# First cross-attention of a four-layer decoder: key steps issued in pairs instead of one by one

## The chip, the cores and the metric

The kernel runs on one core of a Trainium2 chip. The metric is the device time of one execution in microseconds (us). The core's engines work side by side, each through its own instructions in order, and wait for one another by semaphores: TensorE (PE, with its weight loads PEld) multiplies matrices into PSUM; VectorE (DVE) and ScalarE (ACT) read PSUM and SBUF; GpSimd (POOL) works on SBUF alone; SyncE (SP) issues most transfers. Changes of under 0.2% cannot be told from no change here.

## The reference, cut to what matters

A decoder of four layers; each has self-attention, cross-attention over a context of 6404 keys, and a feed-forward block. The change is in the cross-attention of the first layer alone: 1024 queries, 16 heads of 64, all 6404 keys, float32.

```python
qw = (q_in @ Wq + bq).reshape(B, M, HEADS, QSIZE)
kw = (k_in @ Wk + bk).reshape(B, N, HEADS, QSIZE)
vw = (v_in @ Wv + bv).reshape(B, N, HEADS, KSIZE)
a = jnp.einsum('bmhd,bnhd->bhmn', qw, kw) / jnp.sqrt(jnp.float32(QSIZE))
a = jnp.where(key_mask[:, None, None, :], a, -jnp.inf)
a = jax.nn.softmax(a, axis=-1)
o = jnp.einsum('bhmn,bnhd->bmhd', a, vw).reshape(B, M, HEADS * KSIZE)
return o @ Wo + bo
```

Here q_in is the normalised x, and k_in and v_in are the context; the result is added to x.

## The kernel before

The work of the stage (`l0_xattn`, L675 on) is cut into 64 **units**: 16 heads by 4 blocks of W = 256 queries. The keys lie in two halves of 3202 (HALF), each half on 64 of the 128 partitions of kS. A unit goes through the keys in NSTEP = 13 **steps**; a step takes two runs of 123 or 124 keys (`key_step`, L574) from each half, four in all, so its scores are 123 or 124 partitions by 1024 columns (two banks of PSUM, tile s, two buffers); such a set of scores is called a **strip** below.

The softmax runs in two passes. In the first, a step's scores are made, joined to a running maximum, and copied to SBUF (tile p, 18 buffers). When all 13 are there the maximum over the keys is found; in the second pass, 15 steps later (NS + LAG), each slot has its maximum subtracted, is raised to the exponential, summed, and multiplied with the values. So one turn of the loop over a, in `l0_xattn`, issues scores of one unit and the second pass of the unit before. The instructions of a turn:

- `scores` (PE, all at helper line L275): for each of two runs, and in each of both halves of the rows, a float32 product of kS and q with 256 columns (two records each), then a bfloat16 product of the mask row `drop` with ones, which adds a large negative number to dropped keys. The two halves of the rows work as separate 64-row tiles.
- `lowered` (DVE L771): slot plus the negated maxima, which stand in PSUM (tile neg). `raised` (ACT L776): the exponential in place. `summed` (POOL L785): the slot is added to tot; after the last step tot is folded once, to 512 columns (toth, L788).
- `kept`: the running maximum (DVE L735, reads s and most), then the copy from s to p (ACT L737).
- after the last step of a unit `halved` (DVE L742) folds the maximum to 512 columns; one turn later `turned` transposes it on PE (L751) and reduces it on DVE (L754), and `spread` (PE L763), two turns after the halving, puts the negated maxima of the queries on all partitions.
- `weighted` (PE, L275): the values of the step before, acc<-p,v, in 64-column tiles; eight records. After a unit's last step `taken` (ACT L809) copies acc to oT, and two steps later `onto` makes the denominators (m<-ones,toth, eight records) and the output product (m<-w_head,oT); DVE takes the reciprocal (rd, L826) and adds the result to x (L829).

Beside this stand, at set turns, the keys of the next head (`head_keys`, seven chunks, ACT L598), its queries (two, ACT L700), and in the last unit of every second head the values of the next two heads (`pair_values`, one a step, ACT L617). These, `turned` and `onto` share two PSUM buffers of tile m.

The order is written out by hand: every instruction of the loop goes through `pin` or `matmul`, which keep it in program order on its engine. `pool.tile` hands out the buffers of a tag in turn; an instruction that writes a buffer waits until the earlier readers are done.

Of the kernel before, what the change touches and what calls it, by code (L numbers as in the profile page):

```python
# [218 lines left out]
class Decoder:  # L219
# [354 lines left out]
    def key_step(self, i):  # L574

        n = 124 if i < 2 else 123
        return (248 * i if i < 2 else 496 + 246 * (i - 2)), n
# [8 lines left out]
    def head_keys(self, w):  # L586

        nc, H = self.nc, self.HALF
        k = self.keys_pool.tile([P, H], F32, tag="kS", name="kS", bufs=2)

        def chunks(psum):
            for c in range(0, H, BANK):
                n = min(BANK, H - c)
                m = psum()
                for s in range(2):
                    self.matmul(m[64 * s:64 * s + 64, :n], lhsT=w[:, 128:192], rhs=self.ctxT[:, s * H + c:s * H + c + n],
                                start=True, stop=True, tile_position=(0, 64 * s))
                self.pin(nc.scalar.activation(k[:, c:c + n], m[:, :n], AF.Identity, bias=w[:, 321:322]))  # L598
                yield

        return k, chunks
# [7 lines left out]
    def pair_values(self, w, i, m):  # L609

        c, n = self.key_step(i)
        v = self.keys_pool.tile([P, 4, P], F32, tag=f"v{i}", name="v", bufs=1)
        for s in range(2):
            for j in range(2):
                a = s * self.HALF + c + j * n
                self.matmul(m[:n, (2 * s + j) * P:(2 * s + j + 1) * P], lhsT=self.ctxT[:, a:a + n], rhs=w, start=True, stop=True)
# [3 lines left out]
    def first_keys(self, ps, pool):  # L620
# [10 lines left out]
        self.drop = kp.tile([P, self.HALF], BF16, tag="drop", name="drop")  # L631
        nc.gpsimd.memset(self.drop, 0.0)
        for s in range(2):
            nc.sync.dma_start(out=self.drop[64 * s:64 * s + 1, :],
                              in_=line.rearrange("t p -> (t p)")[s * self.HALF:(s + 1) * self.HALF][None, :])
        self.one16 = kp.tile([P, self.WQ], BF16, tag="one16", name="one16")
        nc.gpsimd.memset(self.one16, 1.0)
# [37 lines left out]
    def l0_xattn(self):  # L675
# [6 lines left out]
        NH, NB, NS, W, H = 16, S // self.WQ, self.NSTEP, self.WQ, self.HALF  # L682
        LAG, LIVE = 2, 18
        units = NH * NB
        with tc.tile_pool(name="b", bufs=2) as pool, tc.tile_pool(name="b_ps", bufs=2, space=PSUM) as ps0:
# [25 lines left out]
            def scores(a):  # L711

                u, i = divmod(a, NS)
                _, k, q = heads[u // NB]
                c, n = self.key_step(i)
                qs = slice(u % NB * W, u % NB * W + W)
                s = ps.tile([P, 2, BANK], F32, tag="s", name="s")
                for j in range(2):
                    ks = slice(c + j * n, c + j * n + n)
                    for lhs, rhs, first in ((k, q[:, qs], True), (self.drop, self.one16, False)):  # L720
                        for t in range(2):
                            r = slice(64 * t, 64 * t + 64)
                            mm(s[:n, t, j * W:(j + 1) * W], lhsT=lhs[r, ks], rhs=rhs[r, :], start=first, stop=not first)
                return s

            def kept(a, s):

                u, i = divmod(a, NS)
                n = self.key_step(i)[1]
                p = pool.tile([P, 2 * BANK], F32, tag="p", name="p", bufs=LIVE)  # L730
                flat = s.rearrange("p t c -> p (t c)")
                if i == 1:
                    most[u] = pool.tile([P, 2 * BANK], F32, tag="most", name="most")
                if i:
                    pin(nc.vector.tensor_tensor(most[u][:n], flat[:n], (most[u] if i > 1 else slots[a - 1])[:n], ALU.max))  # L735
                slots[a] = p
                return lambda: pin(nc.scalar.copy(p[:n], flat[:n]))  # L737

            def halved(u):

                mh = pool.tile([P, BANK], F32, tag="half", name="half", bufs=1)
                pin(nc.vector.tensor_tensor(mh[:124], most[u][:124, 0:BANK], most[u][:124, BANK:], ALU.max))  # L742
                del most[u]
                most[u] = mh

            def turned(u):

                m = psum()
                for b in range(2):
                    for j in range(2):  # L750
                        pin(nc.tensor.transpose(m[:, b * W + j * P:b * W + j * P + 124],  # L751
                                                most[u][:124, j * W + b * P:j * W + (b + 1) * P], self.ident[:124, :124]))
                r = pool.tile([P, 2], F32, tag="r", name="r")
                pin(nc.vector.tensor_reduce(r, m.rearrange("p (b j k) -> p b j k", b=2, j=2)[:, :, :, :124], AX.XY, ALU.max,  # L754
# [11 lines left out]
            def lowered(b):  # L766

                u, i = divmod(b, NS)
                n = self.key_step(i)[1]
                p = slots[b][:n].rearrange("p (t c) -> p t c", c=W)  # L770
                pin(nc.vector.tensor_tensor(p, p, negs[u][:n, None, :W].to_broadcast([n, 4, W]), ALU.add))  # L771

            def raised(b):

                n = self.key_step(b % NS)[1]
                pin(nc.scalar.activation(slots[b][:n], slots[b][:n], AF.Exp))  # L776

            def summed(b):

                u, i = divmod(b, NS)  # L780
                n = self.key_step(i)[1]
                if i == 1:
                    tots[u] = pool.tile([P, 2 * BANK], F32, tag="tot", name="tot")
                if i:
                    pin(nc.gpsimd.tensor_tensor(tots[u][:n], slots[b][:n], (tots[u] if i > 1 else slots[b - 1])[:n], ALU.add))  # L785
                if i == NS - 1:
                    th = pool.tile([P, BANK], F32, tag="toth", name="toth", bufs=1)
                    pin(nc.gpsimd.tensor_tensor(th[:124], tots[u][:124, 0:BANK], tots[u][:124, BANK:], ALU.add))  # L788
                    tots[u] = th

            def weighted(b):

                u, i = divmod(b, NS)
                n = self.key_step(i)[1]
                h = u // NB
                if i == 0:
                    accs[u] = ps.tile([P, BANK], F32, tag="acc", name="acc")
                v, p, e = values[h // 2][i], slots[b], 64 * (h % 2)
                for j in range(2):
                    for t in range(2):  # L800
                        at = (2 * t + j) * W
                        mm(accs[u][64 * t:64 * t + 64, :W], lhsT=v[:n, 2 * t + j, e:e + 64], rhs=p[:n, at:at + W],
                           start=i == 0 and j == 0, stop=i == NS - 1 and j == 1, tile_position=(0, 64 * t))
                slots.pop(b - 1, None)
# [7 lines left out]
            def onto(u, oT):  # L812
# [4 lines left out]
                for b in range(2):  # L817
                    for j in range(2):
                        mm(m[:, W + b:W + b + 1], lhsT=th[:124, j * W + b * P:j * W + (b + 1) * P], rhs=self.ones[:124, 0:1],
                           start=j == 0, stop=j == 1)  # L820
                for b in range(2):
                    mm(m[:, b * P:(b + 1) * P], lhsT=oT[:, b * P:(b + 1) * P], rhs=w[:, 192:320], start=True, stop=True)
                rd = pool.tile([P, 2], F32, tag="rd", name="rd")

                def add():
                    pin(nc.vector.reciprocal(rd, m[:, W:W + 2]))  # L826
                    for b in range(2):
                        x = self.x[:, u % NB * 2 + b, :]
                        pin(nc.vector.scalar_tensor_tensor(x, m[:, b * P:(b + 1) * P], rd[:, b:b + 1], x, ALU.mult, ALU.add))  # L829

                return add

            keys, asked, vw = iter(()), iter(()), None
            out = None
            total = units * NS
            for a in range(total + NS + LAG + 3):
                u, i = divmod(a, NS)
                b = a - NS - LAG
                ub, ib = divmod(b, NS)
                h, at = divmod(a, NB * NS)  # L840
                if a < total and h + 1 < NH:
                    if at == 2:
                        w = self.head_weights(h + 1)
                        k, gen = self.head_keys(w)
                        keys = gen(psum)
                        qn, asked = queries(w)
                        heads[h + 1] = (w, k, qn)
                    if at >= 6 and at % 5 == 1:
                        next(keys, None)
                    if at in (44, 48):  # L850
                        next(asked, None)
                s = scores(a) if a < total else None
                if 0 <= b < total:
                    lowered(b)
                    raised(b)
                    summed(b)
                copy = kept(a, s) if a < total else None
                if copy:
                    copy()
                if a < total and i == NS - 1:  # L860
                    halved(u)
                if u > 0 and i == 0 and u <= units:
                    turned(u - 1)
                if 0 <= b - 1 < total:
                    weighted(b - 1)
                    pu, pi = divmod(b - 1, NS)
# [1147 lines left out]
```

## Time and profile before

| what | us |
|---|---|
| median of 3 runs | 5793.36 (5789.67 to 5799.3) |
| the profiled execution | 5792.23 |
| its span, first to last instruction | 5790.1 |
| stretch of the first cross-attention, from the first p copy on | 284 to 2633 |

| engine, whole span | busy us | share |
|---|---|---|
| PE | 5373.4 | 93% |
| PEld | 2453.1 | 42% |
| DVE | 3767.8 | 65% |
| ACT | 3801.8 | 66% |
| POOL | 2256.3 | 39% |

Costs of one instruction in the stretch, by the view of groups and the tile views:

| line, engine | what | mean ns | times |
|---|---|---|---|
| L735 DVE | most<-s,most, 1024 columns | 1224 | 704 |
| L771 DVE | p<-p,neg, 1024 columns | 1210 | 832 |
| L737 ACT | p<-s, 1024 columns | 1011 | 832 |
| L776 ACT | p<-p (exponential), 1024 columns | 1059 | 832 |
| L785 POOL | tot<-p,tot, 1024 columns | 2398 | 704 |
| L788 POOL | toth<-tot, 512 columns | 1274 | 64 |
| L742 DVE | half<-most, 512 columns | 1276 | 64 |

And of the same kinds elsewhere in the profile: L451 DVE p<-s,neg, 512 columns, 692; L452 ACT exponential, 512 columns, 630; L456 POOL tot<-tot,p, 512 columns, 1266.

How to read it: a share of busy time is a mean over the whole kernel, of which the first cross-attention is some 40%. The line L275 is that of a helper, so PE's products are told apart by their tiles. Durations of PE overlap with one another, so its costs are read as distances from start to start. The chain of waits ends in later layers and passes through this stage by PE.

### The profile page before, as it was taken

The numbers are of one execution on the slowest core, as the hardware profiler recorded it, in microseconds if no ns is written. First come the engines' busy times: TensorE is split into PE (matmuls) and PEld (weight loads), VectorE is DVE, ScalarE is ACT, GpSimd is POOL, SyncE is SP. The second block draws the span as 40 slices with busy tenths as digits, with TensorE's granted clock in tenths as the row PEclk, the third lists the DMA queues.
The fourth block names the chain that finished last, engine by engine and source line by source line (L and its number), as shares of the span: only waits on it lengthen the run. The fifth ranks groups of instructions, "written<-read, shape, count | busy, mean of one in ns | idle before, by whom it ended". The sixth has DMA issues, their size and how long they took to land. (4 is left out here: it accounts for less than half of the span.)

```text
span 5790.1 us, 89326 instructions
## 1 busy us (share of the span) xinstructions
PE 5373.4 (93%) x36760; PEld 2453.1 (42%) x36760; DVE 3767.8 (65%) x4507; ACT 3801.8 (66%) x4975; POOL 2256.3 (39%) x1089
## 2 busy tenths in 40 slices
PE   6899999999999999998999589999997699999999
PEld 3355555565656565654854232111144111111136
DVE  5588888888888888882354622000035999999913
ACT  2477777778787777772223258999901188888772
POOL 1078887878788888782325301000001000000000
PEclk8899999999999999998999779999998599999999
DMA  3000000000000000001000133000033000000000
GB/s 106 1 1 2 3 2 3 2 3 2 3 3 3 2 2 2 1 1 49 6 11 1 62 91 95 10 9 1 9 120 103 1 8 16 16 9 1 1 12 26
DMA packets 67724, 115.74 MB, mean 20 GB/s; under 512 B 10748, under 2 KB 50018, under 8 KB 65908
## 3 DMA queue, kind: packets, MB, share of 16 engines
q1 hardware_dynamic: 66740, 106.76, 5.9%
q8 instruction: 288, 4.72, 0.3%
q10 hardware_dynamic: 576, 3.28, 0.2%
q14 instruction: 120, 0.98, 0.1%
HBM read 78.56 MB, written 31.42 MB: 19 GB/s over the span
## 5 line engine op out<-in xcount | busy, mean ns | idle before, releaser
L785 POOL TENSOR_TENSOR tot<-p,tot 123x1024 f32<-123x1024 f32 x704 | 1688.3, 2398 | 309.1 <-ACT p L776 265.7
L275 PE MATMUL acc<-p,v 123*64 123x256 f32 (+4 forms) x9896 | 1326.2, 458 | 25.1 <-ACT oT L809 20.3
L1382 DVE TENSOR_REDUCE mx<-m 128x2 f32<-128x1024 f32 (+4 forms) x928 | 1027.1, 1157 | 94.1 <-PE m L275 84.5
L275 PE MATMUL s<-q,kS 64*123 64x256 f32 (+1 forms) x6656 | 1031.1, 401 | 11.9 <-ACT p L737 11.3
L776 ACT ACTIVATE p<-p 123x1024 f32<-123x1024 f32 (+1 forms) x832 | 881.0, 1059 | 210.4 <-DVE p L771 187.2
L771 DVE TENSOR_TENSOR p<-p,neg 123x1024 f32<-123x1024 f32 (+1 forms) x832 | 1006.3, 1211 | 16.6 <-PE neg L763 9.9
L737 ACT COPY p<-s 123x1024 f32<-123x1024 f32 (+1 forms) x832 | 841.0, 1011 | 252.9 <-DVE most L735 232.8
L1454 ACT ACTIVATE p<-s 128x512 f32<-128x512 f32 (+4 forms) x1620 | 819.4, 589 | 230.7 <-PE s L275 229.6
L735 DVE TENSOR_TENSOR most<-s,most 123x1024 f32<-123x1024 f32 x704 | 861.4, 1224 | 149.1 <-PE s L275 148.1
L1451 ACT ACTIVATE p<-s 128x1024 f32<-128x1024 f32 x918 | 844.0, 1183 | 31.1 <-PE s L1446 31.0
L275 PEld LDWEIGHTS acc<-p,v 123*64 123x64 f32 (+3 forms) x9896 | 456.4, 121 | 594.7 <-issue 373.3
L275 PEld LDWEIGHTS s<-q,kS 64*123 64x123 f32 (+1 forms) x6656 | 492.3, 182 | 406.5 <-issue 226.6
L1425 PE MATMUL acc<-p,v 128*8 128x512 f32 (+2 forms) x3672 | 622.1, 596 | 0.0
L275 PE MATMUL m<-kP,qP 64*128 64x512 bf16 (+4 forms) x1856 | 369.3, 394 | 111.8 <-DVE mx L1382 57.3
L275 PE MATMUL s<-one,drop 64*123 64x256 bf16 (+1 forms) x3328 | 458.7, 269 | 0.0
L275 PE MATMUL s<-qP,kP 64*128 64x512 bf16 (+4 forms) x1620 | 380.1, 384 | 7.9 <-ACT p L1454 5.3
L785 POOL TENSOR_TENSOR tot<-p 124x1024 f32<-124x1024 f32 x64 | 151.9, 2373 | 352.3 <-ACT p L776 352.3
L1446 PE MATMUL s<-qP,kP 48*128 48x512 bf16 (+2 forms) x1836 | 280.3, 383 | 5.7 <-ACT p L1451 4.9
L281 DVE COPY oT<-acc 128x512 f32<-128x512 f32 x14 | 9.7, 690 | 400.4 <-PE acc L1425 391.1
L275 PEld LDWEIGHTS <-qP 64*128 64x128 bf16 x1856 | 122.3, 96 | 326.5 <-issue 259.0
L400 POOL MEMSET mpad<- 128x512 f32 x2 | 1.1, 526 | 639.9 <-PE m L1535 603.1
L275 PEld LDWEIGHTS <-drop 64*123 64x123 bf16 (+1 forms) x3328 | 231.3, 132 | 43.8
(478 smaller groups left out, 4902.0 us busy)
## 6 DMA issues: line engine op xcount, KB each, us to landing
kd<-part SPq DMA_DIRECT2D x156, 128.0 KB, 1.9
wb<-expert_weights SPq DMA_DIRECT2D x30, 512.0 KB, 3.8
kP<-kd SPq DMA_DIRECT2D x24, 512.0 KB, 4.6
kP<-kd SPq DMA_DIRECT2D x48, 192.0 KB, 4.7
w_expert<-in_Y_w SPq DMA_DIRECT2D x8, 768.0 KB, 4.3
qd<-part SPq DMA_DIRECT2D x36, 128.0 KB, 1.9
qP<-qd SPq DMA_DIRECT2D x16, 256.0 KB, 5.6
ctxT<-in_ctxT ACTq DMA_DIRECT2D x4, 800.5 KB, 7.4
```

The costliest lines, as they stand in the source:

```text
L275: return self.tc.keep_in_program_order(self.nc.tensor.matmul(*a, **k))
L281: self.nc.vector.tensor_copy(out, in_)
L735: pin(nc.vector.tensor_tensor(most[u][:n], flat[:n], (most[u] if i > 1 else slots[a - 1])[:n], ALU.max))
L737: return lambda: pin(nc.scalar.copy(p[:n], flat[:n]))
L771: pin(nc.vector.tensor_tensor(p, p, negs[u][:n, None, :W].to_broadcast([n, 4, W]), ALU.add))
L776: pin(nc.scalar.activation(slots[b][:n], slots[b][:n], AF.Exp))
L785: pin(nc.gpsimd.tensor_tensor(tots[u][:n], slots[b][:n], (tots[u] if i > 1 else slots[b - 1])[:n], ALU.add))
L1382: nc.vector.tensor_reduce(mx[:, t, 2 * pair:2 * pair + 2, c:c + 1], m[:, :, :b - a], AX.X, ALU.max)
L1425: matmul(acc[32 * j:32 * j + v.shape[3], off:], lhsT=v[:n, t, 4 * g + j, :], rhs=ws[j][:n, :BANK - off], start=t == 0, stop=t == nkt - 1, ...
L1446: matmul(ss[j][:n, :w], lhsT=kP[pair][r, t * P:t * P + n], rhs=qP[pair][r, hs], start=True, stop=not diag)
L1451: nc.scalar.activation(p2[:n], both[:n], func)
L1454: nc.scalar.activation(pp[j][:n, :w], ss[j][:n, :w], func)
```

## The change

**Pairs.** The 13 steps of a unit become seven groups: six pairs and the last alone, g0 to g6; bg0 to bg6 are the groups of the second pass. A turn of the loop issues the scores of both steps of a group, then the lowering, the maxima and copies, the raise, the sum, and then the values of both steps of a group. The lag is counted in groups: the second pass comes 8 turns (LAG = NG + 1) after the scores, the values one turn after the raise. Key chunks stand in turns 3, 4, 5, 10, 11, 12 and 17 of a head's 28, queries in 18 and 19; the values of the next heads are made two a turn.

**Slots.** A pair has one slot of 2048 columns (tag pp, 9 buffers); the last step has one of 1024 (tag p, 2 buffers). Lowering, raise and sum take a whole slot in one instruction. The running maximum has one buffer instead of two, and so has tot.

**Mask.** All steps have 124 keys a run (KT). The padding of the first half's last step runs into the second half's keys and is masked; ctxT gets 22 zero columns for the second half's. `drop` holds the mask of a strip's two runs in two rows, and `one16` has ones where row and run agree, so that one product of 512 columns masks a strip. It stands first in the strip, before the float32 products.

**Sums.** tot has 2048 columns and is folded three times, to 1024, 512 and 256 columns; the denominators take two products instead of four.

**Order.** The transposes of the maximum stand between the two strips of the next unit's first group; `spread` stands at the end of that turn; the output product and its addition to x stand at the end of the fourth turn of a unit. In a unit's first group the copies precede the first maximum.

The core of the diff:

```diff
-        LAG, LIVE = 2, 18
+        GROUPS = [(i, i + 1) for i in range(0, NS - 1, 2)] + [(NS - 1,)]
+        NG = len(GROUPS)
+        LAG = NG + 1
...
+            def scores(u, i):
+                _, k, q = heads[u // NB]
                 qs = slice(u % NB * W, u % NB * W + W)
                 s = ps.tile([P, 2, BANK], F32, tag="s", name="s")
+                for t in range(2):
+                    r = slice(64 * t, 64 * t + 64)
+                    mm(s[:n, t, :], lhsT=self.drop[r, i * n:(i + 1) * n], rhs=self.one16[r].rearrange("p j c -> p (j c)"),
+                       start=True, stop=False)
                 for j in range(2):
+                    ks = slice((2 * i + j) * n, (2 * i + j + 1) * n)
+                    for t in range(2):
+                        r = slice(64 * t, 64 * t + 64)
+                        mm(s[:n, t, j * W:(j + 1) * W], lhsT=k[r, ks], rhs=q[r, qs], start=False, stop=j == 1)
...
+            def kept(u, i, s):
+                g, j = divmod(i, 2)
+                if not j:
+                    pair = len(GROUPS[g]) == 2
+                    slots[u, g] = pool.tile([P, (4 if pair else 2) * BANK], F32, tag="pp" if pair else "p", name="p",
+                                            bufs=9 if pair else 2)
+                pin(nc.scalar.copy(slots[u, g][:n, j * 2 * BANK:(j + 1) * 2 * BANK], s[:n]))
...
+                if g == NG - 1:
+                    for w in (2 * BANK, BANK):
+                        pin(nc.gpsimd.tensor_tensor(t[:n, :w], t[:n, :w], t[:n, w:2 * w], ALU.add))
+                    th = pool.tile([P, W], F32, tag="toth", name="toth", bufs=1)
+                    pin(nc.gpsimd.tensor_tensor(th[:n], t[:n, 0:W], t[:n, W:2 * W], ALU.add))
...
+            for a in range(total + LAG + 3):
+                u, g = divmod(a, NG)
+                h, at = divmod(a, NB * NG)
+                bu, bg = divmod(a - LAG, NG)
+                wu, wg = divmod(a - LAG - 1, NG)
+                eu, eg = divmod(a - LAG - 3, NG)
...
+                if live:
+                    ss.append(scores(u, GROUPS[g][0]))
+                if g == 0 and 0 < u <= units:
+                    turn = turned(u - 1)
+                if live and len(GROUPS[g]) > 1:
+                    ss.append(scores(u, GROUPS[g][1]))
+                if 0 <= bu < units:
+                    lowered(bu, bg)
+                for i, s in zip(GROUPS[g], ss):
+                    largest(u, i, s) if i != 1 else None
+                    if turn is not None:
+                        least(u - 1, turn)
+                        turn = None
+                    kept(u, i, s)
+                    largest(u, i, s) if i == 1 else None
...
+                if 0 <= bu < units:
+                    raised(bu, bg)
+                    summed(bu, bg)
+                if live and g == NG - 1:
+                    halved(u)
+                if 0 <= wu < units:
+                    weighted(wu, wg)
+                if live and h + 1 < NH:
+                    if at in (3, 4, 5, 10, 11, 12, 17):
                         next(keys, None)
+                    if at in (18, 19):
                         next(asked, None)
...
+                        for i in GROUPS[wg]:
+                            values[hp + 1].append(self.pair_values(vw, i, psum()))
+                    if wg == NG - 1:
+                        out = wu, taken(wu)
+                if g == 0 and 0 < u <= units:
                     spread(u - 1)
+                if 0 <= eu < units and eg == NG - 1:
+                    added(out[0], onto(*out))
```

## The prediction

> **What bounds the kernel now.** I read the windows view first, for the stretch of the first cross-attention (from the first p copy near 284 us to 2633 us), then the timeline of a quiet stretch in it, then the waits of the same stretch. The windows row gives, after the stretch, the busy us of each engine with its instructions, and the granted clock:
>
> ```profile
> 284.00:2633.00 2349.00, 2285.66 (x18980) 1377.53 (x18976) 2031.47 (x1947) 1834.00 (x1959) 1921.17 (x832) 0.99 0.01 2
> ```
>
> The columns are PE, PEld, DVE, ACT, POOL, then PEclk. PE is busy 97% of the stretch at a clock of 0.99, DVE 86%, POOL 82%, ACT 78%. PE sets the pace, but DVE is close behind, and the timeline shows how close (start, duration):
>
> ```profile
> 1417.19 1.08 PE L275 MATMUL acc<-p,v 123*64 123x256 f32 x8
> 1417.30 1.22 DVE L735 TENSOR_TENSOR most<-s,most 123x1024 f32<-123x1024 f32 x1
> ...
> 1418.20 0.70 PE L275 MATMUL s<-q,kS 64*123 64x256 f32 x4
> 1418.44 1.21 DVE L771 TENSOR_TENSOR p<-p,neg 123x1024 f32<-123x1024 f32 x1
> ...
> 1418.61 1.01 ACT L737 COPY p<-s 123x1024 f32<-123x1024 f32 x1 [0.16 <-DVE most L735]
> 1418.74 0.28 PE L275 MATMUL s<-one,drop 64*123 64x256 bf16 x2
> ...
> 1418.85 0.60 PE L275 MATMUL s<-q,kS 64*123 64x256 f32 x4
> ...
> 1419.28 0.28 PE L275 MATMUL s<-one,drop 64*123 64x256 bf16 x2
> ...
> 1419.48 1.08 PE L275 MATMUL acc<-p,v 123*64 123x256 f32 x8
> 1419.59 1.22 DVE L735 TENSOR_TENSOR most<-s,most 123x1024 f32<-123x1024 f32 x1
> ...
> 1420.50 0.29 PEld L275 LDWEIGHTS s<-q,kS 64*123 64x123 f32 x4 [0.39 <-issue]
> ```
>
> One step is 1418.20 to 1420.50, 2.29 us. DVE holds a max (L735) and a lowering (L771) in it, starting 1.14 and 1.15 apart: DVE has nothing left either. On PE the starts are 0.54, 0.11, 0.43, 0.20 and 1.02 apart. Undisturbed, a strip's f32 half is 0.43 and its mask 0.11, and the values, four passes like two f32 halves, 0.86. So the two changes of array shape per step (64-row scores, 64-column values) cost 0.11 + 0.09 + 0.16 = 0.36 us. The waits view:
>
> ```profile
> DVE most L735 <- PE s L275: 173.0, 226, 4.8
> DVE rd L826 <- PE m L275: 92.8, 63, 4.7
> ACT p L737 <- POOL tot L785: 7.5, 18, 0.7
> ```
>
> DVE waits for PE at the maxima and, 1.5 us a unit, at rd for the output product; slots almost never wait for POOL. A unit (13 steps; the starts of L742 in the trace) takes 34.3 to 35.1 us, 34.7 in the mean, 64 times; where the next heads' values are made, 14.2 us more per two heads. Of 34.7, 29.8 are steps.
>
> **The change, part by part.** The sum is against the profiled execution, 5792.2 us (span 5790.1 and 2.1 around it); the median of the runs is 5793.4.
>
> PE. A pair group has two strips at 0.215 + 0.86 = 1.08 (one mask product of 512 columns instead of two of 256: the same columns, 0.22), values of 1.72 and one pair of shape changes, 0.25 to 0.36 (the mask now stands first, so the f32 weights may load under it): 4.15 to 4.25, against 4.58 for two steps. Per unit, six entries of 0.36 go, and half of the denominator products (0.45, four of eight records of 0.112); the transposes now stand between two strips, one more change, +0.25. PE's sum falls by 2.35 us a unit.
>
> The Trainium skill (TensorEngine Tiling, Key Properties) says that a change of tiling mode drains TensorE, and so speaks for pairs. It gives no price; the 0.36 us above agrees. By it alone the change would give 64 x 2.35 us = 150 us, an estimate; the rest of this sum does not use it.
>
> DVE. A lowering of 2048 columns is not in the trace. The 1024 take 1.21 and the 512 of L451 0.69, so 2048 should take 1.21 + 1.07 = 2.28, and the next may start at 2.20; the ends are 2.20 (a slope as from 512) and 2.42 (two of today's); I take 2.28, since both rows lie on one line. The two maxima of a pair now stand next to each other, and the second reads what the first wrote. Today a lowering lies between. The same dependence is seen from L735 to L742: 1.26 us from start to start (1421.88 to 1423.14), against 1.14 without it. Ends 1.14 and 1.33 (the closest two maxima of the first unit); I take 1.26. A pair: 2.20 + 1.26 + 1.13 = **4.59** us. That is two steps of today (4.58). PE's saving meets a DVE that saves nothing.
>
> ACT. A raise of 2048: 1.06 and 0.63 (L452, 512 columns) give 1.91; ends 1.85 and 2.12. A copy starts 1.26 after the start of its max. From the start D of a group's lowering: maxima at 2.20 and 3.46, second copy 4.72, raise 5.63 to 7.54. The values of that group are issued an iteration later and start at 7.6, that is 3.0 into the next group, and end at 4.9. The next strip is ready at 1.7 in its group, needed at 2.2: slack 0.5. So a plain group holds 4.59.
>
> Now the unit, 7 groups, with D6 = 0 for the group of the last strip.
> - Turn, g6 and g0. Lowering to 2.2, max 3.46, halving to 4.7 (1.26, its median); PE meanwhile: values 3.0 to 4.9, strip 0 to 6.1, transposes to 6.65, strip 1 to 7.85, values to 9.8, then spread, whose result is there at 10.4. The next lowering waits for it, and the second copy and max of g0 (8.05, 9.15) end then too. **10.4** us, against 7.5 of DVE work. Values of a pair stand ahead of spread.
> - g1 to g5: 5 x 4.59 = 22.95.
> - Output product at g3. rd stands on DVE behind the group's last max; its product stands on PE behind values (3.0 to 4.9), a key chunk where there is one (0.95), and itself 1.1, so it is there at 6.15 or 7.1 in the group; rd and the two additions take 0.73. The group is 6.9 or 7.85 instead of 4.59: +2.3, or +3.2 in three units of four; mean **+3.0**. Behind rd waits the next lowering, so all of DVE. Today's like wait costs little, as PE is the bound.
> - Slots at g3. Nine pair slots, six per unit: g3 takes the slot of the previous unit's g0. POOL reads that one only in the addition of bg1 (the second group of the second pass, at g2), which starts when the raise of g2 ends (7.54 after D2). An addition of 2048 is 2.37 + 2.21 = 4.58 (512: 1.27, 1024: 2.37; ends 4.3, 4.75). It ends 7.5 into g3, and the first copy of g3 wanted to start at 3.5. Most hides in the rd wait; the strip of g4 comes 1.0 late: **+1.0**. Ends 0 (if the slot is released sooner) and 1.5.
> - POOL per unit: 5 x 4.58 + 2.37 + 2.37 + 1.27 + 0.71 = 29.6, today 12 x 2.37 + 1.27 = 29.7; within the unit, no bound.
>
> Sum 10.4 + 22.95 + 3.0 + 1.0 = **37.4** a unit, 2.75 more than 34.7: 64 x 2.75 = 176 us. Head-weight loads are issued as before on SP.
>
> Values of the next heads: two a group (2 x 1.05) behind the values products. Two m buffers serve the key chunk and both; the third taker waits for ACT to empty the key chunk, which stands behind the 1.91 raise, so g4 and g5 lose some 4 us each and g3 2 to 5, beside 7 in the groups of the turn: 17 per two heads against 14.2 now, 7 times: +20. Ends 0 and +50.
>
> Set-up: mask rows as 8 DMAs instead of 2, the one-hot rows by two DVE copies instead of a POOL memset, beside the self-attention of the first layer: nothing, up to 3 us if uncovered. End: after the last strip one raise of 1.91 and POOL's three folds (4.35 instead of 1.27): +4.
>
> Total 176 + 20 + 4 = +200: 5792.2 + 200 = **5992 us**.
>
> **Rivals.**
> A. PE stays the bound: unit 34.7 - 2.35 = 32.3, 150 us less: 5642; half of it 5717. For: 97% busy PE, waits of DVE for PE of 173 us. Against: 4.59 on DVE is above 4.25 on PE. It needs DVE to be elsewhere than on the path at rd and at the turn. Chance 0.14.
> B. The waits are partly covered: slots free in time (-1.0), no wait between the maxima (-0.12 x 6), values no dearer: 5992 - 64 x 1.7 - 20 = 5863. The order is written out by hand (pin), so the pairs are issued as said; but the release of a slot is only argued. Chance 0.18, 3 in 18 of it within 0.2%.
> C. The clock. It is 0.99 here; in the page's slices with PE 60 to 80% busy it is 0.8 to 0.9. With PE down to some 31 of 37 us it could fall to 0.85: some 10 us of PE lie on the path of a unit (turn and output product), +1.8 each: 5992 + 115 = 6107. Chance 0.08.
>
> On this the Trainium skill (TensorE: Matmul & The Clock Gate, HAM oscillation) has the clock fall after idle gaps of over about 3.4 us. No gap in the sum above is that long; no run here shows the limit, and C is priced by the slices alone.
>
> **How the numbers follow.** Forecast 0.60, A 0.14, B 0.18, C 0.08. The bounds above (lowering -30 to +54 us, maxima -47 to +27, slot -64 to +32, values -20 to +30), not all at one end together, put the forecast's own range at 5890 to 6080; the range takes in most of B: 5835 to 6085. Under 0.2% (12 us) the runs can't tell a change. Faster 0.14, same 0.03, slower 0.83.
>
> **What would show it.** Right: max to max 1.26 apart, a lowering near 2.28, groups of 4.6 us in the quiet stretch; PE under 90% in the stage; DVE's wait at rd two to three us a unit; a wait of the first copy of g3 for POOL of some 3 us, 64 times; a lowering that waits for spread each unit; clock still 0.99. Wrong: groups under 4.4 us, or L735's counterpart waiting for PE most of the time. The prediction falls if a unit lasts under 34.7 us.

## The result, and the profile after

The changed kernel takes 6175.3 us in the median of 4 runs (6159.0 to 6195.6), the kernel before 5791.5 in the same session: **6.6% slower**, ratio 1.0662 with a 95% interval of 1.0619 to 1.0706. The profiled execution took 6159.5 us, 367 more than that of before. The forecast was 5992, with a range of 5835 to 6085: the direction was right, the loss nearly twice as large.

The windows view of the stage, which now runs to some 2999 us (columns as before: PE, PEld, DVE, ACT, POOL, then the clock):

```profile
284.00:2999.00 2715.00, 2222.69 (x17016) 1475.80 (x17015) 2157.34 (x1559) 1724.79 (x1571) 1903.03 (x574) 0.96 0.01 3
```

The stretch is 366 us longer (2715 against 2349), so the whole loss is here. PE is busy 82% of it instead of 97%, DVE 79% instead of 86%: neither is full, and the units spend their time in waits. The waits view of the same stage:

```profile
ACT p L751 <- POOL tot L803: 246.3, 59, 4.7
PE s L275 <- ACT p L751: 211.4, 120, 3.1
DVE most L742 <- PE s L275: 203.6, 196, 3.7
DVE rd L849 <- PE m L275: 155.0, 63, 9.1
```

The first line is the wait for a slot, 7.5 us before; the fourth is the wait for the output product, 93 before. The timeline of one unit without values of the next heads, in its quiet part (start, duration; the number behind an x joins instructions of one kind):

```profile
1568.56 2.28 DVE L789 TENSOR_TENSOR p<-p,neg 124x2048 f32<-124x2048 f32 x1
...
1570.75 2.55 DVE L742 TENSOR_TENSOR most<-s,most 124x1024 f32<-124x1024 f32 x2
...
1573.21 2.28 DVE L789 TENSOR_TENSOR p<-p,neg 124x2048 f32<-124x2048 f32 x1
...
1579.17 0.17 DVE L849 RECIPROCAL rd<-m 128x2 f32<-128x2 f32 x1 [1.22 <-PE m L275]
...
1579.91 2.28 DVE L789 TENSOR_TENSOR p<-p,neg 124x2048 f32<-124x2048 f32 x1
1580.85 1.93 ACT L751 COPY p<-s 124x1024 f32<-124x1024 f32 x2 [4.70 <-POOL tot L803]
1581.91 0.69 PE L275 MATMUL s<-one,drop 64*124 64x512 bf16 x2 [2.77 <-ACT p L751]
1582.29 2.01 PE L275 MATMUL s<-q,kS 64*124 64x256 f32 x8
...
1584.34 1.23 DVE L742 TENSOR_TENSOR most<-s,most 124x1024 f32<-124x1024 f32 x1 [2.16 <-PE s L275]
...
1587.67 0.43 PE L275 MATMUL s<-one,drop 64*124 64x512 bf16 x2
...
1591.92 0.43 PE L275 MATMUL s<-one,drop 64*124 64x512 bf16 x2
```

A plain group is 4.65 us (1568.56 to 1573.21), as forecast within 0.07; a lowering of 2048 is 2.28. The group with the output product is 6.7 (1573.21 to 1579.91). The next one is 7.1 (1579.91 to 1587.04, the start of the next lowering): its maxima wait for PE, PE waits 2.77 us for the copy, and the copy waited 4.70 us for POOL. A PE group without waits is 4.25 us (1587.67 to 1591.92), also as forecast. The first strip behind the stall takes 2.1 us (1581.91 to 1584.00), twice as long as elsewhere; the last section says why.

The turn that follows in the same timeline:

```profile
1592.05 2.28 DVE L789 TENSOR_TENSOR p<-p,neg 124x2048 f32<-124x2048 f32 x1
...
1595.12 9.50 POOL L803 TENSOR_TENSOR tot<-p,tot 124x2048 f32<-124x2048 f32 x2 [0.43 <-ACT p L794]
...
1595.49 4.72 DVE L756 TENSOR_TENSOR most<-most 124x512 f32<-124x512 f32 x1
...
1600.14 1.21 DVE L789 TENSOR_TENSOR p<-p,neg 124x1024 f32<-124x1024 f32 x1
1600.27 0.64 PE L763 MATMUL m<-ident,most 124*128 124x124 f32 x4 [2.06 <-DVE most L756]
```

Here stands what the forecast had not: the halving of the maximum (L756), which reads 512 columns of SBUF and another 512 of SBUF, lasts **4.72 us**. It began 0.37 us after an addition of POOL and ended 0.55 us after that addition (the line joins two, of 4.55 and 4.88). The transposes waited for it.

### The profile page after: what moved, and what is told of

The parts are those of the page before. It is cut to its first block, busy times and chain, and to the rows that moved or that the text cites. A ratio compares the mean times of both kernels' runs of the same rounds, so it can differ in the third digit from the quotient of the medians.

```text
span 6157.4 us, 83974 instructions
## 1 busy us (share of the span) xinstructions
PE 5310.9 (86%) x34840; PEld 2549.8 (41%) x34840; DVE 3900.6 (63%) x4125; ACT 3698.3 (60%) x4591; POOL 2238.8 (36%) x834
## 5 line engine op out<-in xcount | busy, mean ns | idle before, releaser
L803 POOL TENSOR_TENSOR tot<-p,tot 124x2048 f32<-124x2048 f32 (+1 forms) x320 | 1335.4, 4173 | 432.0 <-ACT p L794 367.6
L751 ACT COPY p<-s 124x1024 f32<-124x1024 f32 x832 | 835.6, 1013 | 942.8 <-DVE most L742 502.0
L275 PE MATMUL acc<-p,v 124*64 124x256 f32 (+3 forms) x9896 | 1252.5, 456 | 118.4 <-ACT p L794 58.5
L742 DVE TENSOR_TENSOR most<-s,most 124x1024 f32<-124x1024 f32 x704 | 860.8, 1223 | 238.9 <-PE s L275 209.1
L789 DVE TENSOR_TENSOR p<-p,neg 124x2048 f32<-124x2048 f32 (+1 forms) x448 | 952.2, 2126 | 24.6 <-PE neg L779 22.6
L275 PE MATMUL s<-q,kS 64*124 64x256 f32 x6656 | 935.4, 398 | 0.0
L794 ACT ACTIVATE p<-p 124x2048 f32<-124x2048 f32 (+1 forms) x448 | 803.3, 1794 | 12.5 <-DVE p L789 12.4
L275 PEld LDWEIGHTS acc<-p,v 124*64 124x64 f32 (+2 forms) x9896 | 496.2, 123 | 691.0 <-issue 301.9
L275 PEld LDWEIGHTS s<-q,kS 64*124 64x124 f32 x6656 | 717.3, 196 | 72.7 <-issue 0.2
L275 PE MATMUL s<-one,drop 64*124 64x512 bf16 x1664 | 370.8, 429 | 215.7 <-ACT p L751 213.5
```

The costliest lines, as they stand in the source:

```text
L275: return self.tc.keep_in_program_order(self.nc.tensor.matmul(*a, **k))
L742: pin(nc.vector.tensor_tensor(most[u][:n], s[:n], other[:n, 0:2 * BANK], ALU.max))
L751: pin(nc.scalar.copy(slots[u, g][:n, j * 2 * BANK:(j + 1) * 2 * BANK], s[:n]))
L794: pin(nc.scalar.activation(p, p, AF.Exp))
L803: pin(nc.gpsimd.tensor_tensor(t[:n, :w], p, (t[:n, :w] if g > 1 else slots[u, 0][:n]), ALU.add))
```

## The experiments

**The theory** after this reading: a unit is a chain of DVE groups of 4.66 us plus three waits, (1) the halving, blocked by POOL's long addition, (2) the slot of g3, held by POOL, (3) the output product. **The rival**: the time went into PE (a lower clock, dearer shape changes), and the waits cover one another, so that removing one gains little. Below, "D4 to D5" is the time from the lowering issued in the turn of g4 to that in the turn of g5, a median over units of one kind, that is, at the same place in each pair of heads, so that the same key chunks stand beside them.

**e1_half.** The halving reads one operand from PSUM:

```diff
-                t = most[u]
-                pin(nc.vector.tensor_tensor(t[:n, 0:BANK], t[:n, 0:BANK], t[:n, BANK:], ALU.max))
+                t, m = most[u], psum()
+                pin(nc.scalar.copy(m[:n, :], t[:n, BANK:]))
+                pin(nc.vector.tensor_tensor(t[:n, 0:BANK], m[:n, :], t[:n, 0:BANK], ALU.max))
```

> One edit to the changed kernel: before the halving of the maximum, ACT copies the upper half of most to a PSUM buffer (ahead of the last strip's own copy), so that VectorE's halving reads one operand from SBUF and one from PSUM. Theory (the halving stands 4.34 us in the median, 1.26 before, because it reads two SBUF operands and stays blocked until POOL's 4.57 us addition is over): the halving takes about 0.7 us, D6 to D1 falls from 12.44 to about 10.4 us, the kernel from 6159 to about 6030 us (6000 to 6060). Rival (the turn is bounded by PE, values ahead of spread, and the halving is covered): under 20 us gained.

Measured: 6047.5 us, ratio 1.0442 (1.0422 to 1.0462), 128 us under the change. Its timeline, in a turn where POOL is busy throughout:

```profile
1505.70 11.64 POOL L804 TENSOR_TENSOR tot<-p,tot 124x2048 f32<-124x2048 f32 x3 [1.61 <-ACT p L795]
1506.71 0.59 ACT L756 COPY m<-most 124x512 f32<-124x512 f32 x1 [0.56 <-DVE most L742]
1507.33 0.69 DVE L757 TENSOR_TENSOR most<-m,most 124x512 f32<-124x512 f32 x1 [0.71 <-ACT m L756]
```

The halving is 0.69 us under the same POOL load, and in all 64 units (690 to 693 ns). The turn, D6 to D1, is 10.3 us in most units instead of 12.44. The theory holds. The trace of the change alone says the same: its turn is 12.44 us in 41 units, and 10.3 (once 10.7) in the six, without values of the next heads and at full clock, in which the halving happened to take 0.69 us.

**e4_pool.** POOL's additions are cut in two:

```diff
-                    pin(nc.gpsimd.tensor_tensor(t[:n, :w], p, (t[:n, :w] if g > 1 else slots[u, 0][:n]), ALU.add))
+                    for c in range(0, w, 2 * BANK):
+                        cs = slice(c, c + 2 * BANK)
+                        pin(nc.gpsimd.tensor_tensor(t[:n, cs], p[:, cs], (t[:n, cs] if g > 1 else slots[u, 0][:n, cs]), ALU.add))
```

> One edit: POOL adds each pair slot in two instructions of 1024 columns (2.37 us each) instead of one of 2048 (4.57), everything else as changed. Theory (the halving is blocked for the rest of one POOL instruction): the halving falls to 2.4 us at most, 1.3 to 1.8 in the median, and the kernel to about 6060 us (6030 to 6100), though POOL's work is some 0.8 us a unit more. Rival (the halving slows by a share of bandwidth, whatever the length of POOL's instruction): halving still near 4 us, no gain.

Measured: 6043.2 us, 1.0437 (1.0416 to 1.0458). The tile views, min/median/max of the halving in ns, first the kernel before, then the change, then e4_pool:

```profile
L742 DVE TENSOR_TENSOR half<-most x64: 692/1259/2207, 307.4 to 2590.5; 124x512 f32<-124x512 f32 x64
```

```profile
L756 DVE TENSOR_TENSOR most<-most x64: 691/4336/4728, 298.0 to 2954.7; 124x512 f32<-124x512 f32 x64
```

```profile
L756 DVE TENSOR_TENSOR most<-most x64: 692/2164/2797, 296.9 to 2829.7; 124x512 f32<-124x512 f32 x64
```

The block follows the length of one POOL instruction (4.57 and 2.37 us); the median of 2.2 is above the expected 1.3 to 1.8, since the halving meets the beginning of an addition (it starts 0.75 us into it in the median, in both kernels). A share of bandwidth would not halve with it. The single records say it more sharply. In all three kernels, before, change and e4_pool, a halving that starts during an addition of POOL ends 0.55 to 0.58 us after the end of that addition, whatever was left of it (63, 62 and 62 of the 64 halvings); the one in the change that started ahead of an addition took 0.69. So the halving waits for the one instruction that runs, and its 1.26 us before were such a wait as well. The turn of e4_pool is 10.3 us like that of e1_half, although its halving still takes 2.2: the turn has room for that much, and only a longer block is paid for.

**e2_copy.** POOL copies the first pair slot into tot at its own turn, so that no slot is read a turn later:

```diff
-                if g == 1:
+                if g == 0:
                     tots[u] = pool.tile([P, 4 * BANK], F32, tag="tot", name="tot", bufs=1)
-                if g:
...
+                    pin(nc.gpsimd.tensor_copy(tots[u][:n], p))
```

> One edit: POOL copies the first pair slot of a unit into tot at its own turn instead of reading it a turn later as an operand of the first addition, so the slot is free a group earlier; POOL does one more copy of 2048 columns per unit (2.2 us, estimated from 0.61 for 512). Theory (slot wait): the ACT copies' waits for POOL, 246 us in the stage, nearly go; D4 to D5 falls from 6.1 towards 4.8 us; about 6075 us (6045 to 6110). Rival (POOL's added copy lengthens the halving's block or POOL becomes late): no gain or slower, 6150 to 6250.

Measured: 6063.6 us, 1.0469 (1.0451 to 1.0487), 112 us under the change. D4 to D5 and D5 to D6 are 4.66 us in every kind of unit but the one that makes values (5.4 to 7.1 and 4.7 to 5.5 without the edit); the copies' wait for POOL is 9.9 us instead of 246. So the release of a slot, which was only argued in the forecast, is shown. It costs 1.75 us a unit, not 1.0, with what the clock does behind the stall (below).

**e3_late.** The addition of the output product goes behind the next lowering:

```diff
-                    added(out[0], onto(*out))
+                    due = out[0], onto(*out)
...
                 if 0 <= bu < units:
                     lowered(bu, bg)
+                if due:
+                    added(*due)
+                    due = None
```

> One edit: the reciprocal and the two additions of the output product on VectorE move from the end of the fourth turn to behind the lowering of the fifth. Theory: the wait for the output product (155 us in the stage) goes, but the slot wait that it covered takes its place, since the first copy of the fourth group waits for POOL until 7.5 us after that group's start: 20 to 90 us gained, 6070 to 6140 us, and not the 155. Rival (the wait at the reciprocal alone sets the length of the group): 6000 to 6020 us.

Measured: 6166.9 us, 1.0650 (1.0623 to 1.0676): 8 us under the change, within the two intervals. In a unit of one kind D3 to D4 falls from 7.55 to 4.66, and D4 to D5 rises from 6.4 to 9.3. The waits of e3_late:

```profile
DVE most L742 <- PE s L275: 295.6, 214, 3.7
ACT p L751 <- POOL tot L803: 193.0, 45, 4.7
DVE rd L849 <- PE m L275: 49.3, 8, 7.1
```

The wait at rd is down by 106 us, that of the maxima for PE up by 92: the slot wait, which reaches the maxima by way of PE, took its place entirely. The expectation's direction held, its gain of 20 to 90 did not.

**c6_three** and **c12_nolate.** All three waits at once (sums in 1024 columns, of which the first pair is added to itself at its own turn; the halving of e1; the late addition), and the same without the late addition:

```diff
+                t, w = tots[u], 2 * BANK
+                for c in range(w if g == 0 else 0, p.shape[1], w):
+                    pin(nc.gpsimd.tensor_tensor(t[:n], p[:, c:c + w], t[:n] if g else p[:, :w], ALU.add))
```

> Three edits to the changed kernel together, each against one wait: POOL sums into 1024 columns again (the first pair added to itself at its own turn, so its slot is free and no POOL instruction is over 2.4 us), the halving reads its upper half from PSUM by way of ACT, and the addition of the output product stands behind the next lowering. Theory (the four groups of 4.67 us, the turn and these waits are the whole of the stage): a unit is 5 x 4.67 + 0.73 + 10.4 = 34.5 us, as long as before; 5795 us (5760 to 5840). Rival (something else that is slower in pairs, such as a lower clock or dearer shape changes, holds part of the loss): over 5900 us.

> As c6_three, but the addition of the output product stands at the end of the fourth turn again, as in the changed kernel. Theory (the wait at the reciprocal and the slot wait cover each other, so that e3_late alone gained nothing, but with the slot free the wait shows): D3 to D4 is 6.7 to 7.8 us instead of 4.66, D4 to D5 0.7 us less, 1.5 to 2 us a unit more, 5910 to 5950 us. Rival (the wait is covered by another in any case): within 30 us of c6_three.

Measured: c6_three 5815.6 us, 1.0055 (1.0040 to 1.0070); c12_nolate 5903.0, 1.0196 (1.0181 to 1.0211), a little under its band. The three waits are 360 of the change's 384 us. The late addition, worth nothing alone, is worth 87 us here: the two waits had covered each other. Of the rival, dearer shape changes fall, as 24 us are all that is left; a lower clock falls as a cause of its own, since it goes with the waits (last section).

**c8_two.** Two running maxima, so that adjacent maxima are independent; the kernel leaves the maximum of the odd steps out of what is subtracted:

> As c6_three, but with two running maxima, one for the even and one for the odd steps, so that two adjacent maxima don't depend on each other; the maximum of the odd steps is left out of the halving, so only the even steps' maximum is subtracted. Theory (DVE bounds the groups, and the second maximum starts 1.32 us after the first instead of 1.14 because it reads its result): groups of 4.5 us instead of 4.67, some 35 us (20 to 60) under c6_three. Rival (PE, whose pair group is 4.25 us and more with key chunks, or ACT bounds the groups): groups unchanged, under 10 us.

```diff
+                    other = (odd if i % 2 and i > 1 else most)[u] if i > 2 else slots[u, 0]
+                    out = (odd if i % 2 else most)[u]
+                    pin(nc.vector.tensor_tensor(out[:n], s[:n], other[:n, 0:2 * BANK], ALU.max))
```

Measured: 5775.9 us, 0.9975 (0.9962 to 0.9989), 40 under c6_three. DVE's timeline, first c6_three, then c8_two:

```profile
1407.16 2.55 DVE L742 TENSOR_TENSOR most<-s,most 124x1024 f32<-124x1024 f32 x2
1409.62 2.28 DVE L790 TENSOR_TENSOR p<-p,neg 124x2048 f32<-124x2048 f32 x1
1411.82 2.54 DVE L742 TENSOR_TENSOR most<-s,most 124x1024 f32<-124x1024 f32 x2
```

```profile
1398.87 1.22 DVE L745 TENSOR_TENSOR most<-s,most 124x1024 f32<-124x1024 f32 x1
1400.00 1.22 DVE L745 TENSOR_TENSOR odd<-s,odd 124x1024 f32<-124x1024 f32 x1
1401.13 2.28 DVE L793 TENSOR_TENSOR p<-p,neg 124x2048 f32<-124x2048 f32 x1
1403.33 1.22 DVE L745 TENSOR_TENSOR most<-s,most 124x1024 f32<-124x1024 f32 x1
```

Two dependent maxima take 2.55 us together, so the second starts 1.32 after the first; two independent ones start 1.13 apart, and the group falls from 4.66 to 4.46. PE's work is the same in both, so DVE bounds the plain groups.

**c7_turn, c10_keys, c11_spread.** On top of c6_three: spread ahead of the values products and the unit's first maximum ahead of the second copy (c11); key chunks seven turns later (c10); both (c7).

```diff
-                    if at in (3, 4, 5, 10, 11, 12, 17):
+                    if at in (10, 11, 12, 17, 18, 19, 24):
...
+                if g == 0 and 0 < u <= units:
+                    spread(u - 1)
                 if 0 <= wu < units:
                     weighted(wu, wg)
...
                     kept(u, i, s)
-                    largest(u, i, s) if i == 1 else None
```

> As c6_three, and in the turn the spread of the maxima stands ahead of the values products, the first maximum of a unit ahead of the second copy, and the key chunks and queries are issued seven turns later, away from the turns that make the values of the next heads. Theory (the turn is 10.4 us because the next lowering waits for spread behind the values): the turn falls to about 9.2 us, 64 times 1.2, and some 20 us go with the key chunks: 5700 us (5650 to 5760), under the kernel before. Rival (the turn is bounded by the chain halving, transposes, reduction, whatever the order): within 20 us of c6_three.

> As c6_three, with the key chunks and queries of the next head issued seven turns later, away from the turns that make the values of the next two heads. Theory (a value product waits for its m buffer behind a key chunk that ACT empties after the 1.91 us raise): the units that make values lose 3 to 5 us less, 15 to 35 us in all, 5780 to 5800 us. Rival (PE is full in those turns, whatever the order): within 10 us of c6_three.

> As c6_three, with spread ahead of the values products in the turn and the first maximum of a unit ahead of the second copy. Theory: D0 to D1 falls from 5.2 to about 4.2 us in all units, and in the units with values by about 3 us, 60 to 80 us in all: 5735 to 5755 us. Rival (the gain of c7_turn came from the key chunks): under 20 us.

Measured: c10 5787.0, 0.9995 (0.9986 to 1.0004), 29 under c6_three; c11 5764.4, 0.9960 (0.9946 to 0.9974), 51 under, and not 60 to 80; c7 **5727.3**, 0.9897 (0.9882 to 0.9912), 88 under. In c11 D0 to D1 falls from 5.1 to 5.6 us to 4.2 to 4.5, as expected; in the units with values it falls by 2.9, but the next group gives 2.0 of that back. The gains add up: 29 + 51 against 88.

**c9_single.** The change without its pairs: 124 keys, one mask product at the head of the strip, the additional fold, in the order of the kernel before.

> The change without its pairs: steps one by one in the order, slots and lags of the kernel before, but with 124 keys a run, one mask product per strip standing first, and the sums folded once more. Theory (PE's saving per step stops at DVE's two instructions of 2.28 us, and the loss comes from the pairs alone): steps of 2.28 us, denominators 0.45 us a unit cheaper, 5770 us (5740 to 5800). Rival (the mask product of 512 columns or the 124 keys cost something): over 5810 us.

Measured: 5736.0 us, 0.9911 (0.9897 to 0.9926). Its PE timeline:

```profile
1394.55 0.43 PE L275 MATMUL s<-one,drop 64*124 64x512 bf16 x2
...
1396.79 0.43 PE L275 MATMUL s<-one,drop 64*124 64x512 bf16 x2
```

This step of PE is 2.24 us; the commonest distance between two lowerings is 2.26 instead of 2.29, and a unit without values takes 33.3 to 34.4 us instead of 34.3 to 35.1. So these parts of the change gain 52 us, and the time lies under the expected 5740 to 5800; the pairs, with their long slots and their order, cost some 440. Even with the waits and the order mended, the pairs show no gain over single steps: the intervals of c7_turn (0.9882 to 0.9912) and c9_single overlap. No run adds the two maxima of c8_two to c7_turn.

## Why the prediction was wrong, point by point

- **DVE bounds a pair**: right. 4.59 forecast, 4.66 measured. The dependent maxima start 1.32 apart and not 1.26, near the upper bound of 1.33; c8_two shows the dependence itself. PE's group of 4.25 was right, and no use.
- **The turn, 10.4 us**: the failed step. It took the halving as "1.26, its median". That median was no cost of the operation but a wait for POOL instructions of 2.4 us: alone the halving takes 0.69, the tile view of before already had it from 692 to 2207 ns, and the spread over equal instructions was the sign. The change made POOL's instruction 4.57 long and the halving 4.34, more than the turn has room for, and the turn became 12.44. Without the block it is 10.3 (e1_half): the rest of the sum was right. The term: 2.1 us in most units; e1_half gives 128 us of the kernel back, part of which is the clock's: it has 36 stretches at half the granted clock (last section) instead of 59.
- **The output product**: right. 6.9 and 7.85 forecast, 6.7 to 7.8 measured.
- **The slots**: the mechanism was right (3 us forecast for the copy's wait, 4.2 measured: 246.3 over 59 times). The price was right where the clock stays full, and too small where it does not. The changed kernel has both in units of one kind; D4 to D6 of units 26 and 34 (the clock is the number behind POOL's count; two plain groups are 9.32):

```profile
1421.17:1431.65 10.48, 8.11 (x70) 5.73 (x71) 9.21 (x8) 8.55 (x7) 6.50 (x3) 1.00 0.00 0
1757.20:1769.09 11.89, 9.89 (x72) 7.34 (x71) 9.20 (x8) 8.59 (x7) 7.07 (x3) 0.86 0.00 1
```

The first is 1.2 us over two plain groups, with 1.0 forecast; the second is 2.6 over. In the two kinds in which both occur, ten units at full clock take 10.4 to 10.5 us and six with a stretch at half clock 11.6 to 11.9, so the stretch costs some 1.2. It falls there in 44 of the 56 units that make no values: 44 x 1.2 = 53 of the 112 us of e2_copy are the clock's, an estimate from these rows. The forecast had no term for it. That this wait and the one at rd cover each other was used in the forecast, and e3_late against c12_nolate shows it.

- **Values of the next heads, 17 us per two heads**: right. Units of the two places take 54.4 and 42.05 us, against 41.0 and 38.0 without: 17.5.
- **POOL "within the unit, no bound"**: true of its sum (29.6) and still the cause of the largest miss: not POOL's load but the length of one instruction counted.
- The sum: from the first halving to the last a unit takes 42.17 us in the mean, values included, and 36.24 before: 5.93 more, where the forecast had 2.75 and 0.3 for the values. Of the 2.9 that are missing, the turn is some 1.9 (41 units 2.1 longer, seven with a stretch at half clock in the turn 3.7) and the clock behind the slot wait some 0.8 (53 us over 63 units), both estimates.
- Rivals: A falls with the result, in which PE is busy 82% and a plain group takes 4.65 us. B falls too: the slots were not free in time (246 us of waits), and the second maximum does wait for the first. C had a fall of the clock, at the wrong place and by the wrong amount: not 0.85 throughout, but 0.50 after stalls and 0.96 in the mean of the stage.

The Trainium skill (SBUF — State Buffer, Who interferes with whom) says that a VectorE instruction with two SBUF inputs contends with a GpSimd instruction that reads SBUF, through a shared read interface, and calls the shared port pair an exclusive lock. The halving's 4.34 and 2.16 us with two SBUF inputs, and its 0.69 with one in PSUM, agree.

## What to carry to other kernels

An engine's own instruction may be a wait in disguise: where equal instructions differ threefold in one trace, ask what else runs beside the long ones, before the median is carried into a sum. Making an instruction of one engine longer lengthens every wait and every buffer hold that depends on its end, here from 2.37 to 4.57 us at a time. When two waits cover each other, removing either alone shows nothing; remove them together before a cause is struck off.

## What the runs showed of the hardware that was not expected

The PE clock. Windows of the changed kernel around the stall shown above (the stretch, its length, then the columns as above; the clock stands behind POOL's count):

```profile
1572.00:1579.00 7.00, 6.85 (x60) 4.52 (x57) 5.78 (x4) 3.83 (x3) 2.71 (x1) 1.00 0.01 2
1579.00:1582.00 3.00, 0.23 (x4) 0.27 (x5) 2.79 (x4) 1.15 (x2) 1.82 (x1) 0.96 0.00 0
1582.00:1585.00 3.00, 3.00 (x16) 2.90 (x17) 0.84 (x2) 2.58 (x2) 0.28 (x1) 0.50 0.00 0
1585.00:1588.00 3.00, 3.00 (x28) 1.82 (x26) 2.67 (x3) 1.86 (x2) 3.00 (x1) 0.98 0.00 0
```

After 2.77 us without a matmul the granted clock is 0.50 for one stretch of 3.4 us, and a strip takes 2.1 us instead of 1.1. Between 320 and 2950 us the clock record of the changed kernel has 59 such stretches, 201 us in all; in the same part of the stage before, c6_three and c9_single have none, and no gap between matmuls is over 1.9 us there. The Trainium skill (TensorE: Matmul & The Clock Gate; HAM oscillation) tells of idle gaps over about 3.4 us; here the longest gap ahead of a stretch was 1.6 to 2.8 us in 52 of the 59 cases. Not every gap is followed by a stretch: of 19 gaps of 2.8 us 13 were, of 49 of 2.1 us seven, and no run here shows what decides it.

The DVE dependence, forecast at 1.26 us: of two maxima of 1024 columns the second starts 1.32 us after the first if it reads its result, 1.13 if it does not.
